# Two transformer blocks on one core: one column of ones in the values, a fifth tile of keys and of values, unread products in TensorE's waits, and a new order of issue

## The chip, the core and the metric

The kernel runs on one core of a Trainium2 chip. The core has TensorE for products (PE; its weight loads appear as PEld), VectorE (DVE), ScalarE (ACT), GpSimd (POOL) and SyncE (SP), which here issues every DMA. The metric is the device time of one execution in microseconds (us), lower is better. All data are 32-bit floats.

## What is computed

The input is x (16 batches of 256 tokens by 256 channels), a vector of conditions per batch, and a context of 256 tokens per batch. Cut to what matters:

```python
# block 1; m = silu(cond) @ w_ada + b_ada, nine pieces of 256 columns
h = ln(x) * (1 + sc_msa) + sh_msa
x = x + self_attn(h) * g_msa            # windows of 128, rolled by 64, 16 heads of 16
h = ln(x) * (1 + sc_mca) + sh_mca
x = x + topk_cross_attn(h, ctx) * g_mca # only the 16 largest of 256 scores enter the softmax
h = ln(x) * (1 + sc_mlp) + sh_mlp
x = x + swiglu(h) * g_mlp               # 256 -> 2 x 1024 -> 256
# block 2: cross attention of x to the context, both normalized and
# scaled and shifted by columns of silu(cond) @ Wss
out = x + cross_attn(ada_ln(x, Wss_q), ada_ln(ctx, Wss_kv)) @ Wp + bp
```

## The kernel before

**A planner writes the order.** The function `pixart_two_blocks` records every step as an `Op` of a `Plan`: its engine, an assumed cost, the tiles it reads and writes, and the function that emits its instructions. The steps of one batch have the parts "self", "prep", "topk", "mlp" and "last", and the table `DUE` gives each step a due time in thousandths of a batch period, written out by hand or by a search. `Plan.order` sorts all steps by due time, so that several batches are interleaved, and walks through them with its assumed costs (`SWITCH`, `OWN`, `LAG`, and for DMAs `ISSUE`, `BEGIN`, `LAND`, `RATE`, `OPEN`) to decide which of a kind's tiles each buffer takes. `Plan.run` emits the steps in that order, and each engine works through its own list strictly in that order.

**Tiles.** The dictionary `shapes` gives the number and shape of the tiles in SBUF, among them four of keys `k2` and four of values `v`. Kind "W" are the eight banks of PSUM of 128 x 512 floats, which take every product.

**The steps by line** (lines of the kernel before, as the profile has them):

- L351, L357, L368 load x and context; L647 loads a weight; L693 loads 256 columns of an ada weight into a tile `rest`. L377 reads a gate's row, spread over the partitions, from a small buffer in DRAM that L751 has written.
- L425 and L427 are the statistics of a normalization, L432 to L434 its scales on GpSimd, L437 the normalized `xn`; L449 transposes it on TensorE, and L463 evicts it as `xT`.
- L475 makes queries and keys, L511 values; L486, L497 and L514 evict them. L558 projects, L888 and L915 are the two products of the MLP, L898 to L908 what lies between on ScalarE and GpSimd.
- L780 (self) and L932 (last) are scores for a maximum, which L588 takes; L598 transposes the maxima to `nmT`, and L605 sends them in 8 small DMAs for each of two chunks into the query tile. L788 and L944 are the scores again, lowered and with keys on the partitions; L612 takes their exponentials.
- L827 is the top-k scores. L846, L854, L866 and L871 find and mark the 16 largest on VectorE, L859 takes exponentials, L875 on GpSimd multiplies mark and exponential to `prT`; L525 transposes it, and L528 evicts it.
- L581 (`weighted`) multiplies values with weights. Four heads go side by side into four groups of 32 rows of a bank. A head's values in `v` are 16 columns, followed by 16 columns of ones that L336 sets once, so that rows 16 to 31 of each group hold the sum of the weights. L538 transposes the bank in blocks of 32 x 32, L540 takes the reciprocal of column 16, L541 divides on GpSimd, L548 transposes back.
- L404 multiplies a projection's weight by a gate's row, L384 adds the row of biases to x.

**Conditions.** `conditioned` makes silu of the conditions and transposes it to `condT` (two chunks of 128 x 16). `ada_columns` (L703) multiplies each 256 columns of an ada weight by it, ten times in all near the start, and L709 and L711 add biases. `gate_rows` (L744) does the same for the three gates with `condT` as the stationary operand. L724 and L764 fold biases of values into a projection's bias.

The last batch (15) is worked in two halves of 128 tokens, which finish one after the other.

Of the kernel before, what the change touches and what calls it, by code (L numbers as in the profile page):

```python
# [12 lines left out]
ALU = mybir.AluOpType  # L13
# [3 lines left out]
P = 128  # L17
# [11 lines left out]
NW = 32  # L29
# [5 lines left out]
        -3027, -4397, -3471, -3599, -5098, -3376, -2645, -3084, -3618, -1977, -2570, -3085, -3359, -3247, -5174,  # L35
        -3588, -3596, -431, -695, -157, 8, -3035, -3444, -156, -402, -441, -3589, -3159, -3051, -3086, -3323, 86,
        -376, 159, 26, -148, 29, -158, 334, 377, 516, -136, -3437, 524, -402, 345, -448, 430, 1141, 1178, 1253, 540,
        1078, 1334, 228, -58, 443, -404, 1252, -71, 428, 1557, -57, 507, 841, 302, 299, 483, -230, -210, 96, -72,
        1354, 1417, 985, 1558, 1602, 445, 168, -27, 1258, 1342,
    ),  # L40
    "self0": (
        178, -1268, -3395, -1437, -1529, -1439, -5228, -2475, -56, -5103, -2746, -2747, -5249, -2746, -2706, -2925,
        -2729, -5250, -3573, -3327, -3037, -3016, -3187, -3023, -3039, -2555, -3040, -3039, 43, 140, -202, -1119,
        -1116, -910, -811, 145, -81, -38, -132, 17, 157, -1137, -808, -1336, -976, 254, -472, -362, -105, -363, 431,
        -718, -93,
    ),
    "prep0": (
        -2332, -1084, -15, -1103, -1963, 736, -1918, 514, 308, -228, -1334, -1335, 632, -769, 127, 694, -742,
    ),
    "topk0": (  # L50
        629, -11, 508, -65, -2495, -66, 291, 102, -772, 48, 291, 30, -776, 38, 290, 51, -2533, 90, 49, 468, 67, -2304,
        71, 30, 677, 698, -2305, 24, 93, -61, 708, -2254, 674, 702, -38, 789, -2249, 917, 909, 1267, 743, 1295, -125,
        63, -46, 39, -774, 42, -109, 705, -2577, 778, -97, 749, -2266, 745, -98, 745, -2463, 664, 654, 550, 850,
        -2335, 892, 809, -179, 967, -2308, 757, 903, -180, 969, -2327, 908, 719, -196, 1029, 681, 1073, 1237, 1296,
        847, 1335, 924, 961, 1061, 1120, 904, 914, 986, 1120, 686, 985, 978, 983, 924, 992, 1088, 787, 548, 1160, 893,
        998, 1181, 899, 1120, 1159, 1138, 1206, 1183, 998, 1008, 1106, 1004, 838, 1212, 950, 1085, 1192, 781, 1207,
        1244, 1255, 1232, 1293, 1161, 1159, 982, 890, 1096, 782, 1049, 1224, 900, 1184, 933, 1240, 894, 1216, 1140,
        1231, 886, 1224, 1217, 1032, 1206, 737, 1227, 1216, 752, 1198, 738, 1221, 1262, 858, 1287, 848, 1200, 1233,
        783, 1224, 810, 1326, 1299, 1222, 711, 1338, 723, 1099, 849, 1380,
    ),  # L60
    "self1": (
        -3478, -4042, -805, -510, -4612, -2278, -2316, -2237, -4112, -2262, -390, -1118, -3568, -3569, -1018, -2976,
        -3569, -395, -2322, -692, -1489, -1465, -682, -1456, -353, -1219, -1461, -1477, -1495, -1344, -161, -627,
        -165, -3303, -3251, -3334, -3335, -47, -57, 32, 68, 101, -299, -2850, -3108, -3088, -3253, -247, -186, 6,
        -1156, 83, -18, -16, 128,
    ),
    "prep1": (
        -4084, -4257, -17, 53, 102, -42, -411, 147, 218, 181, 36, 33, 206, -260, 510, 225, 282,
    ),
    "topk": (  # L70
        94, 53, 163, 160, 4, 121, -38, 55, -63, 145, -59, 66, 184, 59, -366, 67, 109, 463, -23, 372, 645, 559, 48,
        269, -313, 408, -161, 248, 353, 281, 408, -99, 373, -12, 392, 487, -206, 659, 476, 675, 182, 715, 463, -23,
        499, -47, -199, -24, 504, 82, 263, -22, 545, -475, 2, -451, 531, -453, 268, -421, -453, 561, 667, 565, 225,
        -487, 599, 775, 405, 592, 438, 668, 782, 652, -599, 692, 711, 781, 421, 836, 643, 846, -287, 927, 656, 739,
        712, 799, 836, 747, 417, 768, 859, 606, -19, 673, 566, 625, 195, 477, 684, 541, 942, 30, 1043, 790, 757, 902,
        26, 1047, 722, 784, 775, 756, 905, 863, 693, 718, 757, 907, 775, 1097, 1077, 1166, 825, 1182, 849, 956, 790,
        947, 751, 946, 791, 945, 879, 915, -152, 1008, 1103, 943, 792, 993, 874, 992, 1055, 390, 1120, 1069, 979, 955,
        -104, 1070, 1107, 1011, 972, 968, 1130, 1088, 993, 1010, 633, 1117, 1113, 1176, 1065, 1114, 964, 1201, 391,
        1238, 706, 1108,
    ),  # L80
    "self": (
        -1722, -443, -1198, -804, -2008, -1876, -1546, -1510, -950, -1210, -765, -667, -1033, -1065, -675, -624,
        -1069, -679, -1276, -593, -1090, -1091, -1115, -1012, -430, -1599, -1523, -1474, -1475, -1556, -865, -440,
        -308, -386, -445, -600, -603, -212, -219, -461, -1332, -185, -208, -478, -361, -315, -362, -158, -384, -446,
        -1376, -94, -423, -188, -953,
    ),
    "prep": (
        -23, 5, -310, -291, 112, 73, 257, -32, -1133, -1111, -1134, -3, -291, 405, 25, -209,
    ),
    "last": (  # L90
        1047, 1071, 1127, 1163, 1124, 1206, 712, 1303, 932, 999, 1381, 866, 2035, 1757, 1739, 1723, 2103, 2108, 2222,
        2149, 1885, 2182, 2205, 2121, 1997, 2108, 2080, 2268, 1996, 2015, 2066, 2065, 2014, 2284, 2287, 2028, 2226,
        1991, 2271, 2366, 2356, 2353, 2354, 2141, 1901, 2213, 2403, 1838, 1963, 2116, 2117, 2437, 2000, 2148, 2379,
        2458, 1833, 2404, 1968, 1877, 2530, 2091, 1631, 2565, 1630, 2532, 2446, 2359, 1777, 2068, 2559, 1500, 1410,
        2598, 2600, 2353, 2406, 2302, 2304, 2658, 2404, 2403, 2194, 2680, 2764, 2475, 2722, 2485,
    ),
    "mlp": (
        1494, 1306, 703, 702, 1361, 1433, 838, 1532, 1486, 1250, 1255, 1513, 1352, 1542, 1571, 1599, 1480, 869, 876,
        1488, 1420, 1529, 1359, 1415, 1520, 1197, 863, 1541, 1052, 1568, 1365, 1567, 1554, 1160, 1057, 1670, 1621,
        1724, 1029, 1709, 1814, 1620, 1616, 1553, 1150, 633, 1853, 1121, 1875, 1826, 1793, 1880, 1776, 869, 1898, 941,  # L100
        1609, 1300, 1303, 1625, 1530, 1560, 1531, 1525, 1829, 947, 932, 1677, 1535, 625, 1615, 624, 1989, 1963, 1766,
        1664, 893,
    ),
    "self15": (
        -1970, -648, -1706, -864, -1672, -2110, -1485, -1035, -2085, -1469, -710, -1217, -976, -689, -810, -1331,
        -670, -962, -412, -567, -648, -649, -677, -545, -509, -518, -239, -893, -998, -432, -907, -216, -458, -322,
        -1198, -169, -191, -594, -651, -564, -606, -158, -189, -224, -1271, -89, -174, -108, -1155, -2020, -1743,
        -493, -117, -97, -514, -47, -175, -176, -85, -148, -226, 106, 111, 32, 9, -666, -439, -29, -481, -571, -549,
        253, 149, -73, 249, -74, 317, 269, 257, 330, 323, 162, 60, -269, -4, 69, 211, 72, -4, 335, 413, 434, -56, 352,
    ),  # L110
    "prep15": (
        -81, -120, 34, -136, -399, 69, -211, -438, -39, -1166, -1149, 17, -568, -1106, 38, -400, 459, 424, 409, 523,
        9, 546, 533, 14,
    ),
    "topk15": (
        56, -306, 25, 48, 170, -288, -9, -86, 110, 142, 112, 97, 206, -87, -313, -87, 122, -241, 178, 233, 297, 268,
        152, 238, 161, 510, -5, 154, 322, 369, 534, 580, 153, 151, 106, 269, 215, 671, -599, 572, 189, 878, 421, 389,
        377, 441, 88, 404, 251, 461, 73, 489, 390, 507, 589, 157, 364, -324, -18, 360, 490, -68, 738, 554, 513, 534,
        578, 832, 559, 505, -196, 599, 743, 650, 535, 499, 563, 652, -223, 1019, 1046, 1048, 420, 1209, 601, -563,
        -608, 726, 1012, -512, -647, -604, 898, -605, 551, -517, 984, 745, 436, 884, -224, 763, 575, 340, 1090, 997,  # L120
        -677, 920, 398, 1144, 1115, 972, 782, 454, 1116, 1148, 831, 863, -1632, 1114, 1162, 1194, 1272, 498, 473,
        1296, 1040, 1022, 362, 880, 1006, 963, 452, 1229, 1234, 993, 476, 989, 1113, 1042, 435, 1169, 1195, 990, 981,
        423, 1117, 1009, 1223, 410, 579, 1334, 835, 1047, 1087, 363, 1359, 1297, 1249, 461, 706, 1356, 1052, 1417,
        1140, 1200, -360, 990,
    ),
    "last15": (
        -1505, 17, -219, 55, 280, 1060, 1078, 1157, 1267, 1164, 1161, 1306, 483, 994, 987, 629, 1631, -1051, 1973,
# [51 lines left out]


class Op:
    __slots__ = ("tag", "eng", "cost", "hold", "own", "kb", "emit", "due", "mode", "takes", "uses", "after", "start", "end", "n")


class Plan:
# [910 lines left out]
```

## Time and profile before

| | |
|---|---|
| median of 3 runs | 1362.93 us (1361.81 to 1365.57) |
| profiled execution: own time, span of its instructions | 1365.2 us, 1363.1 us |
| busy in the span: PE, PEld, DVE, ACT, POOL | 1327.1, 1040.8, 1216.9, 1014.4, 1026.4 us |
| mean granted TensorE clock | 0.981 |
| instructions | 38514 |

A busy time is the time in which an engine has at least one instruction in work. PEld overlaps PE. A line of the order of time has start, length, engine, line, operation, output and inputs, shapes and count; a wait of the engine before it stands in brackets with what ended it. TensorE takes each 32-bit product in two passes, so one product of the code is two rows of the profile, while a transpose is one.

### The profile page before, as it was taken

The numbers are of one execution on the slowest core, as the hardware profiler recorded it, in microseconds if no ns is written. First come the engines' busy times: TensorE is split into PE (matmuls) and PEld (weight loads), VectorE is DVE, ScalarE is ACT, GpSimd is POOL, SyncE is SP. The second block draws the span as 40 slices with busy tenths as digits, with TensorE's granted clock in tenths as the row PEclk, the third lists the DMA queues.
The fourth block names the chain that finished last, engine by engine and source line by source line (L and its number), as shares of the span: only waits on it lengthen the run. The fifth ranks groups of instructions, "written<-read, shape, count | busy, mean of one in ns | idle before, by whom it ended". The sixth has DMA issues, their size and how long they took to land.

```text
span 1363.1 us, 38514 instructions
## 1 busy us (share of the span) xinstructions
PE 1327.1 (97%) x13464; PEld 1040.8 (76%) x13464; DVE 1216.9 (89%) x4357; ACT 1014.4 (74%) x2359; POOL 1026.4 (75%) x1552
## 2 busy tenths in 40 slices
PE   8699999999999999999999999999999999999996
PEld 6466787878778787877878787787878777787875
DVE  3699999999999999999999999999999999998734
ACT  4256778877777878777787878778787877877773
POOL 2456887878788787878878787787878787878752
PEclk9788999999999999999999999999999999999998
DMA  5412000101000010100001010001101000000000
GB/s 158 147 53 58 18 25 18 40 18 41 16 20 25 19 40 18 41 17 18 25 22 37 17 41 18 18 25 22 36 18 41 25 18 25 26 2 10 10 2 18
DMA packets 64161, 42.44 MB, mean 31 GB/s; under 512 B 37764, under 2 KB 56752, under 8 KB 63712
## 3 DMA queue, kind: packets, MB, share of 16 engines
q1 hardware_dynamic: 63967, 39.99, 10.9%
q8 instruction: 107, 1.75, 0.5%
q14 instruction: 87, 0.70, 0.2%
HBM read 35.14 MB, written 4.29 MB: 29 GB/s over the span
## 4 chain that ended last, share of the span: by engine, by line
PE 87%; DVE 5%; POOL 2%; DMA 2%; SPq 1%; issue 1%; ACT 1%; ACTq 0%; POOLq 0%; DVEq 0%
PE W L888 17%; PE W L475 11%; PE W L581 11%; PE W L525 8%; PE W L915 7%; PE W L511 6%; PE W L558 6%; PE W L944 5%; PE W L932 5%; PE W L827 5%; PE W L449 3%; PE W L788 3%; PE W L780 2%; DVE rest L854 1%; DVE rest L871 1%
## 5 line engine op out<-in xcount | busy, mean ns | idle before, releaser
L875 POOL TENSOR_TENSOR prT<-rest,prT 128x512 f32<-128x512 f32 x256 | 325.7, 1273 | 63.5 <-DVE rest L871 49.8
L859 ACT ACTIVATE prT<-W,ntop 128x256 f32<-128x256 f32 x512 | 216.8, 510 | 76.0 <-POOL ntop L848 64.3
L588 DVE TENSOR_REDUCE nm<-W 128x2 f32<-128x512 f32 (+1 forms) x384 | 236.9, 681 | 28.1 <-PE W L932 16.0
L888 PE MATMUL W<-xT,w_L_xcond_w_m 128*128 128x256 f32 (+1 forms) x1088 | 249.0, 375 | 1.5 <-ACT xT L463 1.5
L612 ACT ACTIVATE pTO<-W 128x512 f32<-128x512 f32 (+1 forms) x392 | 200.5, 613 | 62.0 <-PE W L944 37.6
L888 PEld LDWEIGHTS W<-xT,w_L_xcond_w_m 128*128 128x128 f32 x1088 | 189.1, 190 | 57.0 <-ACT pTO L612 10.9
L854 DVE MATCH_REPLACE8 rest<-top,W 128x256 f32<-128x256 f32 x512 | 208.2, 416 | 0.2 <-issue 0.2
L871 DVE MATCH_REPLACE8 rest<-top,rest 128x256 f32<-128x256 f32 x512 | 205.5, 409 | 0.0
L846 DVE MAX8 top<-W 128x8 f32<-128x256 f32 x512 | 187.0, 417 | 14.7 <-PE W L827 14.5
L866 DVE MAX8 top<-rest 128x8 f32<-128x256 f32 x512 | 187.3, 410 | 0.0
L525 PE MATMUL W<-ident,prT 128*128 128x128 f32 x1024 | 144.4, 279 | 11.1 <-POOL prT L875 11.1
L528 ACT ACTIVATE pTT<-W 128x512 f32<-128x512 f32 x256 | 148.4, 621 | 8.8 <-PE W L525 8.7
L541 POOL TENSOR_TENSOR on<-tr,rec 128x128 f32<-128x128 f32 (+1 forms) x162 | 71.0, 443 | 98.6 <-DVE rec L540 98.2
L525 PEld LDWEIGHTS W<-ident,prT 128*128 128x128 f32 x1024 | 120.3, 143 | 32.6 <-POOL prT L875 14.6
L905 POOL TENSOR_TENSOR mb<-ma,mb 128x256 f32<-128x256 f32 (+1 forms) x136 | 94.7, 697 | 62.7 <-ACT mb L903 50.6
L538 DVE STREAM_TRANSPOSE tr<-W 128x256 f32<-128x256 f32 (+1 forms) x162 | 79.2, 490 | 48.1 <-PE W L581 40.1
L915 PE MATMUL W<-w_L_xcond_w_m,h 128*128 128x256 f32 x512 | 113.8, 380 | 0.0
L581 PE MATMUL W<-pTO,v 128*32 128x128 f32 (+1 forms) x2112 | 108.1, 329 | 2.3 <-ACT pTO L612 2.0
L915 PEld LDWEIGHTS W<-w_L_xcond_w_m,h 128*128 128x128 f32 x512 | 95.9, 190 | 13.6 <-POOL prT L875 0.8
L908 POOL TENSOR_TENSOR h<-h,mb 128x256 f32<-128x256 f32 (+1 forms) x136 | 94.8, 697 | 8.3
L581 PEld LDWEIGHTS W<-pTO,v 128*32 128x32 f32 x2112 | 57.8, 111 | 42.6 <-ACT h L907 10.2
L903 ACT ACTIVATE mb<-W,half 128x256 f32<-128x256 f32 (+1 forms) x136 | 69.6, 513 | 9.7 <-PE W L888 8.4
(126 smaller groups left out, 2675.2 us busy)
## 6 DMA issues: line engine op xcount, KB each, us to landing
gate<-gates SPq DMA_DIRECT2D x48, 256.0 KB
q<-nmT SPq DMA_DIRECT2D x480, 1.0 KB
cx<-in_ctx_dram SPq DMA_DIRECT2D x19, 256.0 KB
cx<-in_ctx_dram SPq DMA_DIRECT2D x104, 32.0 KB
rest<-in_L_xcond_w_ada_dram SPq DMA_DIRECT2D x9, 256.0 KB
x<-in_x_dram SPq DMA_DIRECT2D x16, 128.0 KB
x<-in_x_dram SPq DMA_DIRECT2D x32, 64.0 KB
w_L_xcond_w_m<-in_L_xcond_w_m_dram SPq DMA_DIRECT2D x1, 2048.0 KB
```

The lines of the kernel that those rows point to most:

```text
L525: nc.tensor.transpose(w.t[:, ts(n, P)], flat[:, ts(n, P)], ident)
L581: nc.tensor.matmul(po.t[ds(NW * j, NW), ds(q0, nq)], v.t[:, kt, 8 * m + 2 * j + a, :], pT.t.rearrange("p n q -> p (n q)")[:, ds(part, nq)] ...
L588: op("DVE", 0.61, lambda j=j, s=s: nc.vector.tensor_reduce(nm.t[:, k, ds(j, groups, step=4)], s.t.rearrange("p (g k) -> p g k", g=groups), ...
L612: op("ACT", 0.24 + q * 0.0005, lambda s=s, pT=pT: nc.scalar.activation(pT.t.rearrange("p n q -> p (n q)")[:, :q], s.t[:, :q], AF.Exp), r=[ ...
L846: nc.vector.max(top.t[:, a, 0:8], s.t[:, ts(a, L)])
L854: nc.vector.match_replace(rest.t[:, a, :], top.t[:, a, 0:8], s.t[:, ts(a, L)], TAKEN)
L859: nc.scalar.activation(pr.t[:, a, :], s.t[:, ts(a, L)], AF.Exp, bias=ntop.t[:, a:a + 1])
L866: nc.vector.max(top.t[:, a, 8:16], rest.t[:, a, :])
L871: nc.vector.match_replace(rest.t[:, a, :], top.t[:, a, 8:16], rest.t[:, a, :], TAKEN)
L875: op("POOL", 1.25, lambda: nc.gpsimd.tensor_tensor(pr.t, rest.t, pr.t, ALU.mult), r=[rest, pr], w=[pr])
L888: nc.tensor.matmul(w.t[:, :q], w_m1.t[:, c, ds(n0, P)], xT.t[:, c, :q], start=c == 0, stop=c == NCC - 1)
L915: nc.tensor.matmul(pp.t[:, ts(k, C)], hs[f].t[:, ts(k, P)], w_m2.t[:, f, :], start=f == 0, stop=f == NHC - 1)
```

## The change

- `v` holds 17 columns for each head, 16 values and a single one, and `weighted` writes 17 of the 32 rows of each group; the other rows of the bank keep what they held, and nothing of them is used. L336 sets one column.
- Five tiles instead of four of `k2` and of `v`.
- `condT` is 128 columns wide, of which 16 are set and the others are zero, and `ada_columns` moves all 128.
- `Plan.order` looks, before each step of TensorE, at how long TensorE would wait by its own reckoning. Over 1.0 us it puts products of the identity with itself (128 x 512) ahead of the step, into a free bank that nobody reads, as many as fit by 0.87 us each. The built program has 13 of them, at 11 places: five among TensorE's first steps up to the second L558, and eight after the last L915.
- `ISSUE` is 0.53 for 0.47, `LAND` 0.4 for 1.0, and the cost of the ada product 0.9 for 1.7. All of `DUE` is new, so the order of all engines is another, the DMAs of SyncE included.

The number of instructions is the same apart from the 13 products, a memset of `condT` and a fifth memset of `v`.

```diff
-    "start": (-3027, -4397, -3471, -3599, -5098, ...
+    "start": (-9570, -11657, -12085, -9792, -11847, ...
...
-ISSUE, BEGIN, LAND, RATE, OPEN = 0.47, 0.9, 1.0, 320.0, 8
+IDLE, FILLER = 1.0, 0.87
+ISSUE, BEGIN, LAND, RATE, OPEN = 0.53, 0.9, 0.4, 320.0, 8
...
             o.start = t
+            if o.eng == "PE" and t - free["PE"] > IDLE and free["PE"]:
+                ok = slots["W"][:1]
+                n = int((t - max(free["PE"], ok[0][0]) - 0.15) / FILLER) if ok else 0
+                if n > 0:
+                    slot = slots["W"].pop(0)[1]
+                    insort(slots["W"], (t, slot))
+                    o.fill = self.tiles["W"][slot], n
...
+            if o.fill:
+                self.filler(*o.fill)
             o.emit()
...
-        "k2": (4, [P, NCC, 2, L]), "v": (4, [P, NT, NH, NW]), ...
+        "k2": (5, [P, NCC, 2, L]), "v": (5, [P, NT, NH, DH + 1]), ...
...
-        nc.gpsimd.memset(t[:, :, :, DH:NW], 1.0)
+        nc.gpsimd.memset(t[:, :, :, DH:], 1.0)
...
+    def filler(t, n):
+        for _ in range(n):
+            nc.tensor.matmul(t, ident, ident.unsqueeze(1).to_broadcast([P, 4, P]), start=True, stop=True)
+    plan.filler = filler
...
-                    nc.tensor.matmul(po.t[ds(NW * j, NW), ds(q0, nq)], v.t[:, kt, 8 * m + 2 * j + a, :],
+                    nc.tensor.matmul(po.t[ds(NW * j, DH + 1), ds(q0, nq)], v.t[:, kt, 8 * m + 2 * j + a, :],
...
-    condT = fixed("condT", [P, NCC, B])
+    condT = fixed("condT", [P, NCC, P])
+    nc.vector.memset(condT.t, 0.0)
...
-                    nc.tensor.matmul(pm.t[:, ts(m, B)], w.t[:, c, ts(m, P)], condT.t[:, c, :], start=c == 0, stop=c == NCC - 1)
-        op("PE", 1.7, emit, r=[w, condT], w=[pm], mode=128)
+                    nc.tensor.matmul(pm.t[:, ts(m, P)], w.t[:, c, ts(m, P)], condT.t[:, c, :], start=c == 0, stop=c == NCC - 1)
+        op("PE", 0.9, emit, r=[w, condT], w=[pm], mode=128)
```

## The prediction

> **What bounds the kernel now.** I read the page first, then busy time by stretches, the order of time on TensorE, the waits and the chain that ended last.
>
> ```profile
> PE 1327.1 (97%) x13464; PEld 1040.8 (76%) x13464; DVE 1216.9 (89%) x4357; ACT 1014.4 (74%) x2359; POOL 1026.4 (75%) x1552
> ...
> PEclk9788999999999999999999999999999999999998
> ```
>
> TensorE is busy 97% of the span, and its granted clock is full except near both ends. The stretches (us, then busy time of PE, PEld, DVE, ACT, POOL, then granted clock) show where it is not:
>
> ```profile
> 15.40:32.40 17.00, 16.64 (x165) 13.63 (x164) 7.61 (x22) 11.68 (x25) 0.00 (x0) 1.00 0.33 101
> 32.40:46.10 13.70, 13.70 (x148) 10.38 (x147) 5.05 (x19) 3.96 (x8) 4.20 (x6) 0.50 0.64 192
> ...
> 58.24:168.78 110.54, 95.10 (x893) 71.32 (x894) 103.12 (x410) 70.49 (x163) 75.88 (x111) 0.88 0.16 44
> 168.60:1119.90 951.30, 950.78 (x9842) 749.89 (x9841) 902.95 (x3221) 748.05 (x1717) 765.45 (x1137) 1.00 0.10 26
> ...
> 1325.60:1363.10 37.50, 27.02 (x366) 20.22 (x362) 14.03 (x34) 13.59 (x28) 7.29 (x14) 0.87 0.06 16
> ```
>
> From 168.6 (the first L915, the closing product of an MLP) to 1119.9 TensorE idles 0.5 us: 12 batches of 79.2 us, where only less TensorE work can help. From 58.24 (the first scores of the top-k attention) to 168.78 VectorE is the fuller engine, 103.1 of 110.5 us. Before that neither is full; latency and, from 32.4 to 46.1, half the clock decide. The order of time on TensorE (start, length):
>
> ```profile
> 12.09 5.30 PE L475 MATMUL W<-xT,w_L_xcond_w_qkv 128*128 128x256 f32 x16 [1.60 <-DMA w_L_xcond_w_qkv<-in_L_xcond_w_qkv_dram]
> ...
> 33.79 2.48 PE L581 MATMUL W<-pTO,v 128*32 128x128 f32 x32
> ...
> 58.24 1.14 PE L827 MATMUL W<-k,q 32*128 32x512 f32 x8 [0.56 <-ACT q L486]
> 68.24 1.11 PE L525 MATMUL W<-ident,prT 128*128 128x128 f32 x4 [8.86 <-POOL prT L875]
> ...
> 277.82 3.62 PE L475 MATMUL W<-xT,w_L_xcond_w_qkv 128*128 128x256 f32 x16
> 281.36 1.15 PE L932 MATMUL W<-k,q 32*128 32x256 f32 x16
> ...
> 290.73 2.00 PE L888 MATMUL W<-xT,w_L_xcond_w_m 128*128 128x256 f32 x8
> 292.56 0.60 PE L525 MATMUL W<-ident,prT 128*128 128x128 f32 x4
> ```
>
> The same 16 products take 5.30 us at 12.09 and 3.54 (start to start) at 277.82.
>
> **The sum** is made for the span, 1363.1; the profiled execution took 1365.2, the median of the runs is 1362.93. All line numbers are those of before.
>
> *Head, up to the first scores (58.24).* The large transfer of w_qkv was issued at 6.94 and landed at 11.96. Now the context tile and the next batch's x come behind it: it ends after 1564 KB instead of 2076. The first 2076 KB took from about 2.6 to 11.96, so 1564 are in at about 9.6. By then the turned x must be ready: its chain ended at 11.55, and x is issued about 1 us earlier, so 10.5. A filler stands before L475, so I take 10.8: 1.3 us (0 to 2). L475 costs 3.54 instead of 5.30 if fillers and the widened ada products (128 columns moved, not 16) have the clock up: 1.5 of 1.76. Next, from the end of the lowered maxima (nmT, 25.4) to the end of L558 (48.1) took 22.7 us, of which 13.7 at half clock. With steady durations: 16 small DMAs of 0.585 plus 1.44 to land, 10.8; L788 1.0, four exponentials 2.1 and lag, L581 1.0; transposing, reciprocal, division and transposing back 2.4; L558 1.73: 19.2. The gate's row is now written behind all 16 DMAs, not between two groups of 8: 9.4, 1.6 until it can be read back, 3.7 to land (36.1 to 39.85), 1.3 for L404 and 1.27 for L384, with the division L541 queued behind them on GpSimd: about 1.0 late, 20.2. Gain 2.5 (0 to 3.5). From L558 to the first scores the chain is the same; 0.4 comes off because the transposes wait less, an ada product now ahead of the scores included. So the first scores come at 58.2 - 5.7 = 52.5.
>
> *Head, VectorE's part.* Up to the first L915 the same 26 transposed tiles and 8 score groups are asked for in both orders. VectorE had 7.4 us idle. The last row's bias and one ada scale move ahead of the first scores (L764 0.38 and a pair of L709 0.37: 0.7), and of the idle time I take off 1.6 of those waits that were for TensorE: 2.3 (0.7 to 6). Head in all: 8.0.
>
> *Steady batches.* Instructions per batch are the same. Between runs of unlike instructions a gap shows: eight L888 then L525 take 1.83 start to start, where 8 at 0.216 are 1.73. Reading each kind of neighbour so, 72.7 us of work and 6.5 us of gaps make 79.2, what the trace has. The built order has 52 runs a batch for 57. Fewer: product to transpose 8 to 7 (0.055 each), transpose to product 8 to 7 (0.027), transpose to transpose 3 to 1 (0.035), scores to product 8 to 7 (0.216), weighted values to transpose 2 to 1 (0.146), product to product 2 to 1 (0.05); more: scores to transpose 2 to 3 (0.189), weighted values to product 0 to 1 (0.142). Sum -0.23; taken pair by pair -0.26, over 12 batches -3.1. New waits: 0.5 (0 to 4), since even the present order has 0.5 us of them in 951.
>
> *Tail.* L932 at 1336.79 ran at half clock, 3.44 for 1.9, and its first maxima came 1.0 late; a filler ahead of it can hold it up 0.3 (0.87 in a wait of 0.55). The 16 small DMAs behind it on SP (to 1351.09) and the exponentials stay. Gain 0.7 (-1 to 2).
>
> *Priced at nothing.* 13 fillers of 0.87, 5 in the head and 8 in the tail: their cover is TensorE's idle time there (8.86 at 59.4 alone); uncovered, all 13 cost 11.3. A wide ada product: 1.06 for 8 with 16 columns at full clock, about the 1.0 of 8 with 128 would be. The one column of ones: 17 stationary columns for 32.
>
> ```profile
> L581 PEld LDWEIGHTS W<-pTT,v 128*32 128x32 f32 x2048 | 54.4, 110 | 26.0 <-ACT pTT L528 16.8 <-ACT pTO L612 4.3 <-issue 1.8
> ...
> L744 PEld LDWEIGHTS W<-rest,condT 128*16 128x16 f32 x12 | 1.0, 106 | 1.8 <-issue 1.1 <-DVE nm L588 0.2
> ```
>
> Sixteen columns load in 106 ns, 32 in 110, and 16 L581 of 256 take the same 1.0 us as 32 of 128 with twice the loads: loads don't bound it. The shorter memsets of v leave GpSimd idle longer before 6.77, that of condT is one more on an idle VectorE. Fifth tiles k2 and v: no wait of before names them. The Trainium skill (TensorE: Matmul & The Clock Gate, LDWEIGHTS) makes loading go by columns: by it 17 would take an estimated 17/32 of 110, 58 ns; the row of 106 speaks against it, and as loads lie beside products the sum stays either way.
>
> Another rule of that page (Why this matters for your kernels) drops the clock only after gaps of over about 3 us. Here it fell at 32.4 after 17 us with 0.36 us idle, beside an ada product that moves 16 columns; by the rule widening it would bring nothing, the 2.5 above would go, and the sum would be 1354.1.
>
> Sum: 1363.1 - 8.0 - 3.1 + 0.5 - 0.7 = 1351.8; with the 2.1 around it 1353.9 for such an execution, and 11.3 off the median: **1351.6**.
>
> **Rivals.** *Same or little:* VectorE hands the head's gain back. For: it is 93% busy from 58.24 on, and TensorE's 8.86 us wait there is for VectorE and GpSimd, and may drop the clock again (0.50 from 63.2 to 80.2). Against: it starts earlier too. Head 2.0, gaps 1.5: 1359.4. *Slower:* in each steady batch TensorE waits for the product prT (L875) that a merged run of transposes now wants earlier. For: VectorE is 75.2 of 79.2 us busy, 4 us of slack, and runs of 12 transposes stand where 8 and 4 stood. Against: the last of a merged run is asked for only some 0.5 us earlier. The nearest wait is that for xn, 1.7; over 13 batches 22, so 1373.6. It decides from 0.87 us a batch (11.3 / 13). *The clock isn't held:* 1.5 + 2.5 + 0.7 lost, 1356.3, inside my case.
>
> **How the numbers follow.** Mine 0.65, the first rival 0.21, the slower one 0.14. This kernel's measurement tells about 0.3% (4.1 us) from no change, so 1358.8 divides the first rival in two: faster 0.76, same 0.10, slower 0.14. The range: low end with head 12, gaps 3.1, tail 2, about 1345.5, taken to 1344; high end past the first rival to 1361; beyond lies the slower case and a little below.
>
> **What would show it.** First L475 near 10.8 and first scores near 52.5; no half clock around 32 to 46; first L915 near 160.6; batches of 78.9 us between L915s; L932 of the tail under 2 us. Wrong if the first L915 stays above 166, or batches exceed 79.2 with waits for prT in TensorE's list.

## The result, and the profile after

The changed kernel took 1356.09 us (median of 4 runs, 1355.10 to 1358.57), the kernel before on the same chip 1363.43: a ratio of 0.9949, 95% interval 0.9932 to 0.9966. It is faster by 4.6 to 9.3 us, and inside the predicted range; the forecast of 1351.6 was 4.5 too low. The profiled execution took 1355.89, its span is 1354.0. Two lines of the page, busy time and granted clock, stand against the two shown of before:

```profile
PE 1323.4 (98%) x13490; PEld 1029.2 (76%) x13490; DVE 1213.5 (90%) x4358; ACT 1018.0 (75%) x2359; POOL 1026.5 (76%) x1553
...
PEclk9898999999999999999999999999999999999999
```

Busy time by stretches, with the columns of before. The second starts at the first top-k scores, the third at the first closing product of an MLP (now L935), the last at the last one:

```profile
8.30:52.76 44.46, 43.28 (x435) 33.50 (x434) 23.03 (x73) 20.84 (x42) 13.07 (x20) 1.00 0.54 170
52.76:163.90 111.14, 92.46 (x877) 68.39 (x877) 102.82 (x409) 70.76 (x162) 75.61 (x114) 0.92 0.17 54
163.90:1115.20 951.30, 951.30 (x9843) 746.66 (x9843) 900.70 (x3223) 751.06 (x1718) 767.30 (x1137) 1.00 0.10 26
1115.20:1317.80 202.60, 201.66 (x1950) 157.97 (x1948) 170.11 (x607) 159.88 (x407) 159.40 (x254) 1.00 0.04 12
1317.80:1354.00 36.20, 30.09 (x382) 19.86 (x378) 14.03 (x34) 13.60 (x28) 7.75 (x15) 0.99 0.06 17
```

From 8.3 to 52.8 the clock is full throughout. The second stretch, in which VectorE is the fuller engine, is longer than before (111.1 for 110.4), not shorter. The twelve steady batches take 951.3, to the tenth what they took before. TensorE's order of time shows the wait that came in (start, length, what ended the idle time before it):

```profile
10.54 3.70 PE L494 MATMUL W<-xT,w_L_xcond_w_qkv 128*128 128x256 f32 x16
...
52.76 2.53 PE L847 MATMUL W<-k,q 32*128 32x512 f32 x16
62.33 1.24 PE L808 MATMUL W<-q,k 32*128 32x128 f32 x16 [7.04 <-DMA q<-nmT]
64.64 1.24 PE L808 MATMUL W<-q,k 32*128 32x128 f32 x16 [1.08 <-DMA q<-nmT]
66.58 3.52 PE L530 MATMUL W<-w_L_xcond_w_kv,xT 128*128 128x256 f32 x8 [0.70 <-ACT pTO L631]
69.94 1.02 PE L355 MATMUL W<-ident 128*128 128x512 f32 x2
70.80 0.60 PE L544 MATMUL W<-ident,prT 128*128 128x128 f32 x4
...
1329.22 2.01 PE L952 MATMUL W<-k,q 32*128 32x256 f32 x32
```

L808, the lowered self scores of batch 1, waits for small DMAs and stands ahead of the first transposes L544. So those come 18.0 us after the first scores, where L525 came 10.0 after them before, and VectorE, which needs the tiles that they free, stops:

```profile
DVE rest L874 <- ACT prT L879: 2.2, 1, 2.2
```

All stages, with second profiles of both kernels and two variants that the experiments explain (worked out from the starts of the named products):

| us | before | before, again | changed | changed, again | all but the order | sends and joins |
|---|---|---|---|---|---|---|
| to the first scores | 58.2 | 57.0 | 52.8 | 54.2 | 54.4 | 55.1 |
| to the first closing product | 110.4 | 108.1 | 111.1 | 111.0 | 107.1 | 108.1 |
| 12 batches | 951.3 | 951.3 | 951.3 | 951.3 | 951.2 | 950.5 |
| last batches | 205.7 | 205.7 | 202.6 | 202.5 | 205.3 | 202.8 |
| tail | 37.5 | 37.9 | 36.2 | 36.2 | 36.3 | 36.1 |
| span | 1363.1 | 1359.9 | 1354.0 | 1355.2 | 1354.3 | 1352.6 |
| first rise of the clock at | 15.4 | 17.2 | 8.3 | 9.5 | 10.5 | 12.7 |
| half clock from there to the first closing product | 41.0 | 20.5 | 17.1 | 17.1 | 6.8 | 13.7 |
| median of the runs | 1363.43 | 1362.86 | 1356.09 | 1357.12 | 1357.26 | 1352.99 |

### The profile page after: what moved, and what is told of

Same layout as the page of the kernel before. It is cut to its first block, busy times and chain, and to the rows that moved or that the text cites. A ratio compares the mean times of both kernels' runs of the same rounds, so it can differ in the third digit from the quotient of the medians.

```text
span 1354.0 us, 38576 instructions
## 1 busy us (share of the span) xinstructions
PE 1323.4 (98%) x13490; PEld 1029.2 (76%) x13490; DVE 1213.5 (90%) x4358; ACT 1018.0 (75%) x2359; POOL 1026.5 (76%) x1553
## 4 chain that ended last, share of the span: by engine, by line
PE 87%; POOL 2%; DVE 2%; issue 1%; ACT 0%; POOLq 0%; DVEq 0%; ACTq 0%
PE W L908 17%; PE W L494 11%; PE W L600 11%; PE W L935 8%; PE W L544 8%; PE W L577 6%; PE W L530 5%; PE W L964 5%; PE W L952 5%; PE W L847 4%; PE W L468 3%; PE W L808 2%; PE W L800 2%; POOL prT L895 1%; PE W L355 0%
## 5 line engine op out<-in xcount | busy, mean ns | idle before, releaser
L879 ACT ACTIVATE prT<-W,ntop 128x256 f32<-128x256 f32 x512 | 214.0, 497 | 56.0 <-POOL ntop L868 49.1
L908 PE MATMUL W<-xT,w_L_xcond_w_m 128*128 128x256 f32 (+1 forms) x1088 | 251.2, 376 | 0.1
L908 PEld LDWEIGHTS W<-xT,w_L_xcond_w_m 128*128 128x128 f32 x1088 | 187.5, 190 | 61.5 <-ACT pTO L631 13.7
L547 ACT ACTIVATE pTT<-W 128x512 f32<-128x512 f32 x256 | 143.9, 628 | 8.3 <-PE W L544 8.3
L544 PE MATMUL W<-ident,prT 128*128 128x128 f32 x1024 | 137.3, 276 | 6.0 <-ACT prT L879 2.9
L544 PEld LDWEIGHTS W<-ident,prT 128*128 128x128 f32 x1024 | 116.9, 141 | 24.0 <-POOL prT L895 3.8
L560 POOL TENSOR_TENSOR on<-tr,rec 128x128 f32<-128x128 f32 (+1 forms) x162 | 71.7, 444 | 56.2 <-DVE rec L559 54.4
L935 PE MATMUL W<-w_L_xcond_w_m,h 128*128 128x256 f32 x512 | 113.6, 380 | 0.0
L935 PEld LDWEIGHTS W<-w_L_xcond_w_m,h 128*128 128x128 f32 x512 | 97.0, 190 | 13.8 <-POOL mb L925 0.7
L600 PE MATMUL W<-pTO,v 128*17 128x128 f32 (+1 forms) x2112 | 104.9, 323 | 0.1
L868 POOL TENSOR_SCALAR ntop<-top 128x2 f32<-128x2 f32 x256 | 52.7, 217 | 66.1 <-DVE top L866 61.6
L418 POOL TENSOR_TENSOR x<-x,gated 128x512 f32<-128x512 f32 (+1 forms) x49 | 60.1, 1227 | 47.6 <-ACT gated L417 47.5
```

The costliest lines, as they stand in the source:

```text
L544: nc.tensor.transpose(w.t[:, ts(n, P)], flat[:, ts(n, P)], ident)
L600: nc.tensor.matmul(po.t[ds(NW * j, DH + 1), ds(q0, nq)], v.t[:, kt, 8 * m + 2 * j + a, :], pT.t.rearrange("p n q -> p (n q)")[:, ds(part, ...
L879: nc.scalar.activation(pr.t[:, a, :], s.t[:, ts(a, L)], AF.Exp, bias=ntop.t[:, a:a + 1])
L908: nc.tensor.matmul(w.t[:, :q], w_m1.t[:, c, ds(n0, P)], xT.t[:, c, :q], start=c == 0, stop=c == NCC - 1)
L935: nc.tensor.matmul(pp.t[:, ts(k, C)], hs[f].t[:, ts(k, P)], w_m2.t[:, f, :], start=f == 0, stop=f == NHC - 1)
```

## The experiments

Line numbers are those of the kernel named in each. Times are medians; a ratio is to the kernel before on the same chip.

### What holds the clock

**e1, no unread products.**

```diff
-IDLE, FILLER = 1.0, 0.87
+IDLE, FILLER = 1e9, 0.87
```

> The changed kernel without its 13 unread products, all else as it is. If they hold the clock (the prediction's step): the first w_qkv product (16 of L494) runs at half clock as before, 5.3 us instead of 3.54, and the half clock comes back in the tail, where it cost about 1 us each in two places before; the run gets 1.5 to 4 us longer than the 1356.1 of the changed kernel. Rival, the new order alone keeps TensorE's waits short: L494 takes 3.54, no half clock outside 59.5 to 69.7 and 110.7 to 117.5, and the time is 1356.1 or up to 2 us less, since the products that stood at 69.94 (1.02) and 83.12 (1.02) no longer stand ahead of work that was ready.

It took 1358.21, ratio 0.9965 (0.9952 to 0.9978). In the head the rival is right: the clock rose at 10.2, L494 took 3.58 start to start (from its start to that of the next line), the first closing product came at 163.6 (163.9 with them). In the tail the theory is: 38.5 us instead of 36.2, and the order of time shows why.

```profile
1328.42 3.80 PE L952 MATMUL W<-k,q 32*128 32x256 f32 x32 [0.55 <-ACT q L516]
1332.14 3.19 PE L577 MATMUL W<-w_L_xcond_Wp,oT 128*128 128x256 f32 x8
```

L952 takes 3.80 where it took 2.01, L577 3.19 where it took 1.99: half clock from 1327.8 to 1334.6. So the eight products in the tail bring 2.3 us, the five in the head nothing that shows; by times alone the run isn't told from the changed kernel. The other profiles agree: none of the ten with unread products has half clock in the tail before its last 3 us, and the four without (both of the kernel before, e5 and this one) have 6.8 to 10.2 us of it.

**e2, narrow ada products.**

```diff
-nc.tensor.matmul(pm.t[:, ts(m, P)], w.t[:, c, ts(m, P)], condT.t[:, c, :], ...
+nc.tensor.matmul(pm.t[:, ds(m * P, B)], w.t[:, c, ts(m, P)], condT.t[:, c, :B], ...
```

> The changed kernel with the ada products moving 16 columns again instead of 128, all else as it is. If the columns moved hold the clock: it falls to half somewhere between 15 and 46 us for 10 to 14 us, the stretch from the end of the lowered maxima to the end of L577 goes from 20.1 to about 22, the first scores from 52.76 to about 55, and the run gets 1 to 2.5 us longer than 1356.1. Rival, they have no part in it: no half clock before 59.5, first scores at 52.8 within 0.4, the time 1356.1 within 1.

It took 1357.80, ratio 0.9965 (0.9952 to 0.9977); times alone don't tell it from the changed kernel. There was no half clock before 60.3, as the rival said. But the first rise came at 12.5, and the first closing product at 166.0. Over all profiles the first rise came between 7.0 and 12.7 in the ten executions with wide ada products, and at 12.5 (here), 15.4, 17.2 and 17.8 in the four with narrow ones. The last three have the old order and no unread products besides, so for the new order this one run shows no effect of the columns on the rise.

**e3, the old order with unread products and wide ada products.** The change's loop in `Plan.order`, `filler` and `condT`; the old `DUE`, constants, tiles and 32 columns.

> The kernel before, with its own due times, 32 columns and four tiles, and of the change only the unread products and the 128 columns moved by the ada products. If these two hold the clock by themselves: the half clock from 32.4 to 46.1 goes, and the first product over w_qkv takes 3.54 instead of 5.30 although it still starts near 12.1; first scores at 58.24 less 2.5 to 3.5, time 1363 less 2 to 4. Rival, the order does it: half clock around 32 to 46 stays, the time is 1363 within 1.5.

It took 1358.81, ratio 0.9970 (0.9958 to 0.9982): 4.3 us less than before, with the order of the steps as it was. By the reckoning of the old order the planner puts 20 unread products here, not 13: one ahead of the first w_qkv product, eleven around the first top-k scores, eight in the last 75 us.

```profile
9.95 1.02 PE L353 MATMUL W<-ident 128*128 128x512 f32 x2
12.04 3.69 PE L492 MATMUL W<-xT,w_L_xcond_w_qkv 128*128 128x256 f32 x16 [1.06 <-DMA w_L_xcond_w_qkv<-in_L_xcond_w_qkv_dram]
...
55.66 8.85 PE L353 MATMUL W<-ident 128*128 128x512 f32 x20
...
12.00:43.10 31.10, 29.83 (x326) 23.06 (x327) 12.84 (x41) 15.66 (x32) 5.73 (x10) 1.00 0.50 157
```

The first w_qkv product started at 12.04 and took 3.53 start to start, half clock was gone between 9.4 and 70.9, the first closing product came at 162.8 instead of 168.6 (165.1 in the second profile, e11), the tail took 36.3. The theory holds for the two together, and the trace parts them: the clock had risen at 9.4, ahead of the first unread product at 9.95 (in e12 at 10.46, ahead of 10.51). Up to there TensorE's list differs from before by the 128 columns alone, so in the old order the early rise is theirs: two executions against the three at 15.4 to 17.8.

**e11, the kernel before once more**, unchanged.

> The kernel before once more, for a second profile. If the half clock from 32.4 to 46.1 belongs to the kernel (as the prediction took it): some 10 to 14 us of it again between 28 and 46, and 22 to 23 us from the end of the lowered maxima to the end of L558. Rival, it belongs to that execution, since the kernel before with 17 columns and the changed one with narrow ada products showed none there: no half clock between the first rise and 58, and 20.8 us. Either way the first rise comes late (15 to 18) and the first w_qkv product is slow.

It took 1362.86, ratio 0.9999 (0.9991 to 1.0008). Stretches of this second execution, with the columns as above (granted clock third from the end):

```profile
17.20:34.30 17.10, 16.55 (x167) 13.62 (x165) 7.62 (x22) 11.37 (x24) 0.00 (x0) 1.00 0.30 96
34.30:37.70 3.40, 3.40 (x37) 2.21 (x40) 0.62 (x3) 1.16 (x3) 0.00 (x0) 0.50 0.03 7
57.03:165.10 108.07, 91.43 (x892) 68.09 (x893) 103.26 (x410) 69.87 (x163) 75.61 (x111) 0.92 0.18 48
```

The half clock was 3.4 us long here, not 13.7, and it took 20.24 from the maxima to the end of L558, not 22.70. Neither reading was right as put: whether the clock drops there, and for how long, belongs to the execution. In e5, whose first steps are the same but for the 17 columns, it stayed full from 17.8 to 62.2, and the maxima to the end of L558 took 20.8. The late first rise, 15.4 and 17.2 (17.8 in e5), and the slow first product, 5.1 and 6.0 start to start (6.5), are the kernel's.

### What the new order of the head does

**e4, one due time.** Both chunks of batch 1's sends are raised to the due time of the maxima that they carry, 0.640 of a batch before batch 1; the first chunk now comes a thousandth behind the second, whose product TensorE's list has first.

```diff
 DUE["self1"][30]
-  -993
+  -639
```

> The changed kernel with one due time changed, so that the 8 small DMAs of the second chunk of batch 1's lowered maxima, which TensorE's list asks for first, go ahead of the 8 of the first chunk. If the late arrival of these DMAs at 62.33 is what gave back the head's gain: TensorE's wait of 7.04 before L808 falls by about 4.8 (8 issues of 0.6), the first L544 comes at about 66 instead of 70.80, VectorE's wait of 2.25 at 72.87 goes, and the first L935 comes at 161.7 to 162.5 instead of 163.9; the time falls by 1.4 to 2.2. Rival, TensorE's own work from 110 on sets the first L935 (51.6 of 53.9 us busy there): the wait goes and L935 stays at 163.9 within 0.5, the time within 0.7.

It took 1355.48, ratio 0.9942 (0.9927 to 0.9957), not told from the changed kernel by times. Its lines stand 109 earlier (L699 is L808, L435 is L544, L770 is L879):

```profile
55.18 2.53 PE L738 MATMUL W<-k,q 32*128 32x512 f32 x16
60.06 1.52 PE L699 MATMUL W<-q,k 32*128 32x128 f32 x4 [2.35 <-ACT prT L770]
...
71.06 0.60 PE L435 MATMUL W<-ident,prT 128*128 128x128 f32 x4
```

The wait of 7.04 for the DMAs is gone; shorter ones for ScalarE's exponentials L770, which read the banks of the top-k scores, stand in its place (2.35 and 1.0 more). The first L435 comes 15.9 us after the first scores instead of 18.0, VectorE's stop of 2.2 is gone, and from the first scores to the first closing product it takes 109.0 instead of 111.1, with 17 us of half clock in between in both. So the wait cost about 2 us (2.1 against the first profile of the changed kernel, 1.9 against the second). The absolute times missed: in this execution the clock first rose at 11.9, not 8.3, and the scores came 2.4 later.

### What a batch costs

**e5, 17 columns alone**, in the kernel before.

```diff
-"v": (4, [P, NT, NH, NW])
+"v": (4, [P, NT, NH, DH + 1])
...
-po.t[ds(NW * j, NW), ds(q0, nq)]
+po.t[ds(NW * j, DH + 1), ds(q0, nq)]
```

> The kernel before with one thing of the change: 17 columns of values instead of 32, and 17 rows written. In the changed kernel the gap behind each of the 8 runs of weighted values in a batch is 0.012 to 0.013 us shorter than before (64 products, then scores: 1.872 for 1.884). If the 17 columns do that: batches of 79.06 instead of 79.16, 12 of them 1.2 us less, the time 1.2 to 1.6 below 1363. Rival, priced at nothing as on record, since the loads lie beside products: 79.16 stays, the time within 0.5.

```profile
165.60:1115.70 950.10, 949.60 (x9842) 745.64 (x9841) 902.77 (x3221) 749.26 (x1717) 766.54 (x1137) 1.00 0.10 26
```

Batches of 79.06 instead of 79.16, 12 of them 950.1 instead of 951.3: the theory holds. The time was 1360.52, ratio 0.9978 (0.9969 to 0.9988), 1.6 to 4.2 us less; 1.2 lies in these batches.

**e6, four tiles; e7, four tiles and 32 columns**, both in the changed kernel.

```diff
-"k2": (5, ...), "v": (5, ...
+"k2": (4, ...), "v": (4, ...
```

> The changed kernel with four tiles each of keys and values instead of five, in the same order. If the fifth tiles are worth nothing (as on record): batches of 79.25, time 1356.1 within 1. Rival, the new order asks for the fifth tile: a product of keys or values waits for a tile to come free, batches of 79.5 or more, time 3 us or more longer.

> As the run with four tiles, and 32 columns of values instead of 17 (five such tiles of values don't fit). If 17 columns shorten each run of weighted values by 0.0125 us: batches 0.10 longer than with 17 columns, so 79.35 if the four tiles cost nothing, 12 batches 952.4, time 1.2 to 1.6 above the run with four tiles. Rival, no effect: 79.25.

With four tiles: 1355.28, ratio 0.9950 (0.9933 to 0.9966), batches of 79.24. No product waits for a tile; the fifth ones bring nothing. With 32 columns as well: 1357.68, ratio 0.9961 (0.9946 to 0.9976), batches of 79.31. So 17 columns bring 0.07 a batch here and 0.10 in the old order.

**e8, four more joins.** A run is an unbroken row of products or transposes of one line in TensorE's list, a join the place where two runs meet; full shape means weights of 128 x 128. Three due times, in all steady batches.

```diff
 DUE["topk"][25]  462 -> 499
 DUE["topk"][161] 1157 -> 1155
 DUE["mlp"][59]   1704 -> 1713
```

> The changed kernel with three due times of the steady batches altered, so that neighbouring steps with full 128x128 weights change places (one product of L908 with one transpose of L544, one of L530 with one L544, one L544 with one L468): 20 joins between unlike runs of full shape in a batch instead of 16, and the same 32 changes of the weights' shape. By the prices on record (0.027 to 0.055 a join) a batch gets 0.16 longer, 79.42, and 12 batches 2.0. New theory, from both traces: only a change of the shape of the weights costs, a join of two full shapes 0.005: 79.27, the time within 0.6 of 1356.1.

It took 1355.10, ratio 0.9941 (0.9926 to 0.9956), with batches of 79.18: shorter than the 79.25 of the changed kernel, not longer. The prediction's prices fall. The new one, 0.005, fits better and is not all: 0.07 went from one place, eight transposes L544 ahead of four L468, which had 0.130 beyond their steady spacing and now have 0.061.

### What the order is worth, and a version that beats both

**e12, all of the change but the order and the fifth tiles**: e3 with 17 columns.

> The old due times, constants and four tiles with the unread products, the 128 columns moved by the ada products and the 17 columns: all of the change but the order and the fifth tiles. The run with fillers and wide products gave 1358.8 and 17 columns are worth 0.10 a batch: 1357.4, with batches of 79.06. Then the new order is worth 1.3 us in all, its gain of 3.2 in the last batches less 0.19 in each steady one. Rival, the new order carries the change, as the prediction had it with the head's order and the joins: 1359 or more.

It took 1357.26, ratio 0.9963 (0.9950 to 0.9975), as the theory said; the changed kernel beside it (**e10**) 1357.12, ratio 0.9959 (0.9947 to 0.9972).

> The changed kernel itself once more, for a second profile and to stand beside the run with sends and joins. What belongs to the kernel comes again: TensorE's wait of 7.0 before L808, 20.1 us from the end of the lowered maxima to the end of L577, batches of 79.25. What belongs to one execution differs: the clock's first rise anywhere from 7 to 12 us, half clock around 111 to 118 for 3.4 or 6.8 us. Time 1355.5 to 1356.7.

So the new order, with the fifth tiles and its own 13 unread products for the 20 of the old one, is worth 0.1 us, which the runs can't tell from nothing. Stretches of e12:

```profile
54.38:161.50 107.12, 98.19 (x914) 70.35 (x914) 102.79 (x410) 69.57 (x162) 75.56 (x111) 0.97 0.18 49
161.50:1112.70 951.20, 949.97 (x9842) 745.91 (x9841) 902.95 (x3221) 749.50 (x1717) 764.81 (x1137) 1.00 0.10 26
1112.70:1318.00 205.30, 204.94 (x1957) 159.44 (x1955) 170.70 (x606) 160.97 (x410) 159.47 (x255) 1.00 0.04 12
```

The old order is 4.0 shorter from the scores to the first closing product, and 2.7 longer in the last batches. Its eleven unread products around the first scores leave 6.8 us of half clock there, against 17.1 in the changed kernel, but that is not what makes it shorter: with 17.1 in e11 it was 3.0 shorter all the same. In the twelve batches it is level: its undisturbed batch is 79.06, but some reach 79.4 to 80.1.

e10 showed the wait again, the longest in TensorE's list, and its batches were 79.25; the clock rose at 9.5. Its median lies 0.4 above what was expected.

```profile
PE W L808 <- DMA q<-nmT: 8.3, 3, 7.0
```

**e9, the swapped sends and the three due times** in the changed kernel.

> The changed kernel with the swapped sends and the three altered due times together: a version that may beat it. If the two gains seen in the profiles hold (from the first scores to the first closing product 109.0 us instead of 111.1, and batches of 79.18 instead of 79.25, 0.9 over 12): 3.0 less than the changed kernel run beside it, about 1353. Rival, the 2.1 us at the start are lost in the spread with which the clock rises and falls there: 0.9 less, about 1355.

It took 1352.99 (1352.80 to 1354.36), ratio 0.9931 (0.9918 to 0.9945), against 1357.12 for the changed kernel beside it: 4.1 less, and the two intervals don't meet. Its stretches:

```profile
55.14:163.20 108.06, 93.13 (x878) 68.82 (x878) 102.95 (x409) 70.47 (x162) 75.64 (x114) 0.94 0.17 55
163.20:1113.70 950.50, 950.50 (x9843) 746.11 (x9842) 901.00 (x3222) 749.24 (x1718) 765.69 (x1137) 1.00 0.10 26
```

Against the second profile of the changed kernel 2.9 come off ahead of the first closing product (111.0 to 108.1, with 3.4 us less half clock) and 0.8 off the batches. It beats both kernels, and e12 by 4.3, whose interval doesn't meet its own either: an order does pay once that wait is out of it.

## Why the prediction was right or wrong

**Up to the first scores: 52.5 forecast, 52.76 found, and part of it by luck.** The first product was to start at 10.8 and take 3.54; it started at 10.54 and took 3.54. The kernel's second profile has 11.15, and two runs that execute the same instructions up to that point 12.35 and 12.75, where the clock rose at 11.9 and 12.7, so the start belongs to the execution within some 2 us. The length holds in each: 3.45 to 3.58. The third term, 22.7 to 20.2, was found as 20.08 (20.82 in the second profile). But its base was wrong: the kernel before took 20.24 in its second profile, and with 17 columns (e5) 20.8. The step that failed is the gain of 2.5 itself, since what an execution of half clock cost was taken off a median that lay 2.3 below that execution.

**VectorE's part: 2.3 less forecast, 0.8 more found.** Idle time of VectorE grew from 7.4 to 8.3. The step missed that batch 1's sixteen sends and the product that waits for them had moved ahead of the first transposes; e4 priced that at 2.1. The first L935 came at 163.9, not 160.6. At 17 us of half clock each, the old order took 108.1 here, the new one 111.1 and with swapped sends 109.0. The last 0.9 stays open.

**Steady batches: 3.1 less forecast, 0.0 found.** This is the term that was mis-sized most. The joins did fall by five a batch (from 56 runs to 51 in the traces, where the prediction has 57 and 52), but I had priced a join by the class of the two neighbours, as the gap at the end of the first run. Before's own order of time speaks against it:

```profile
262.50 0.66 PE L449 MATMUL W<-ident,xn 128*128 128x128 f32 x4
263.00 1.89 PE L511 MATMUL W<-w_L_xcond_w_kv,xT 128*128 128x256 f32 x8
264.72 1.47 PE L525 MATMUL W<-ident,prT 128*128 128x128 f32 x12
266.03 1.89 PE L475 MATMUL W<-xT,w_L_xcond_Wq 128*128 128x256 f32 x8
```

L511 to L525 takes 1.72, eight spacings of 0.2158 and nothing more: product to transpose is free. The 1.83 of the prediction's L888, also product to transpose, stood behind scores: its 0.10 is the price of coming from 32-row weights, paid in its first product. Sorted by what stands ahead and behind (start to start less steady spacings, over the twelve batches of before), a run of full shape has 0.005 between two others of full shape, 0.093 behind scores, 0.061 behind weighted values, about 0.10 ahead of either, and 0.198 with scores on both sides. Before has 21 joins of full shape a batch, the changed kernel 16, e8 20; changes of shape are 32 in all three. The five joins removed were worth 5 x 0.005 a batch, 0.3 in all.

The page TensorEngine Tiling (Array Packing) of the Trainium skill says under Key Properties that a change of the tiling mode drains TensorE, and a change of tile alone doesn't. The gaps agree: 0.06 to 0.10 us at a change of the weights' shape, 0.005 without.

Then the floor should have fallen, and rose: 79.16, less 0.10 for the columns (priced at nothing, found in e5), less 0.03 for the joins, but 79.25. The missing 0.22 are waits of under 0.1 at a few joins, as L952 to L494 (2.08 for 2.00) and the 0.07 that e8 removed; not all were traced. The term for new waits, 0.5, has its place here: the longer batches of before (up to 79.96), 1.4 together, went, and 2.6 over twelve batches came in small pieces.

**The last batches: nothing forecast, 3.1 found.** The sum left out everything between the thirteenth closing product and the last. The stretch of before, with the columns as above:

```profile
1119.90:1325.60 205.70, 203.92 (x1953) 159.79 (x1951) 170.68 (x606) 160.60 (x410) 159.47 (x255) 1.00 0.05 12
```

TensorE's idle time fell from 1.8 us to 0.9, so 0.8 of the 3.1 can be seen: three times before, two transposes L449 stood directly ahead of the L888 that needs them, twice with a wait for the evicted xT (0.55 and 0.93). Those waits are gone, while new ones for xn, 0.7 together, came in. The 17 columns are worth some 0.2 (e5 has 205.5 there), and the other 2 us were not traced. The old order with the rest of the change has 205.3 (e12), so it is the order.

**Tail: 0.7 forecast, 1.3 found.** Its reason is right: L952 took 2.01 for 3.44. By e1 the unread products bring 2.3, and the new order without them loses 0.6 to 1.0.

**Together** 11.3 were forecast, and the span fell by 9.1, of which 3.1 no step had named; the median fell by 7.3. That the sum comes so near is in part luck: the 3.1 of the last batches stand in for the 3.1 that the steady batches did not bring. Right was that the clock pays: unread products and wide ada products alone bring 4.3. Wrong was that the order does: as built it brings nothing measurable, since what it gains in the last batches it loses before the first closing product. (The low end of the range adds up to 1345.8, not 1345.5, which decides nothing.)

**The rivals.** VectorE did hand gain back, by a DMA wait on TensorE's side. That the clock isn't held did not come about: it was full from 8.3 to 52.8, and in the tail up to the last microsecond. The waits for prT in steady batches did not come: TensorE was busy for all of the 951.3 us, and no wait there reached the 0.87 us a batch that would have decided. Priced at nothing, the fifth tiles were worth nothing (e6).

**The single column of ones: nothing forecast, 1.2 found** over twelve batches in the old order (e5), 0.9 in the new (e7). The prediction set the 106 ns of a load of 16 columns against the 110 of 32. But that 106 is a mean of eight loads at full clock, 96 ns, and four at half clock, 129 (from 44.3 to 45.1 us). The changed kernel has all twelve at full clock:

```profile
L600 PEld LDWEIGHTS W<-pTT,v 128*17 128x17 f32 x2048 | 52.1, 97 | 26.0 <-ACT pTT L547 12.8 <-ACT prT L879 4.6 <-ACT pTO L631 4.3
...
L764 PEld LDWEIGHTS W<-rest,condT 128*16 128x16 f32 x12 | 0.9, 96 | 1.3 <-issue 0.3 <-DVE nm L607 0.2
```

So a load does get shorter with its columns, 13 ns from 32 to 17, and a run of weighted values gets 0.012 to 0.013 us shorter whether it has 16 products or 64. That fits one load in a run that nothing covers; which one was not traced.

**The rule weighed in the prediction.** The prediction took from TensorE: Matmul & The Clock Gate (Why this matters for your kernels) of the Trainium skill that idle gaps of over about 3 us drop the clock, and that by this widening would bring nothing. The fall at 32.4 and the second profile's at 34.3 came after 17 us with 0.36 and 0.55 us idle, against it. Yet with narrow products neither the changed kernel (e2) nor the kernel before with 17 columns (e5) dropped the clock there. What the columns do show, in the old order, is the first rise (e3, e12). The rule's estimate of 1354.1 lay closer to the result than mine, but not for its reason: the 2.5 was missing because its base was.

## What to carry to other kernels

Where a sum is made against one profiled execution, take a second one of the same kernel before calling a slow stretch the kernel's: what one execution lost to the clock is not there to be gained. Price a gap on TensorE by the change of the weights' shape ahead of it and behind it, and count those changes; joins between full-shaped runs cost next to nothing here (0.005 us). Before a mean duration is read as a price, see at which clock its instructions ran. When an order is new, read for each moved product which DMAs it waits for and what stands behind it in its engine's list: one due time cost 2 us of the profile here, and could be had back.

## What the hardware showed

Stretches of half clock are 3.4, 6.8, 10.2, 13.7 and 17.1 us long in these profiles: one to five steps of 3.41. TensorE: Matmul & The Clock Gate of the Trainium skill (Part 1) gives a free-running window of 3413 ns, so that the same kernel warms up at another time in each run; the steps agree, and so do first rises of one program at 8.3 and 9.5, or of another at 15.4 and 17.2.

The mean load of weights took 190 ns for 128 columns of a product (L908), 110 for 32 (L581 of before), 97 for 17 and 96 for 16: some 0.8 to 0.9 ns a column. Seventeen columns for 32 shorten a run of 64 products from 1.884 to 1.872 us and one of 16 from 1.001 to 0.988, although most loads lie beside other work.

Unread products of 128 x 512 can hold the clock through a wait: in e3 ten of them fill the 8.85 us ahead of the first transposes, and the clock stayed full until 70.9, where the kernel before, idle in that wait, fell to half at 63.2 and in its second profile at 61.6.
